# Two attention layers on one core: scores and values in units of eight key chunks, all weights in the common buffer pool

## The chip, the cores and the metric

One core of a Trainium2 chip runs the whole program. The metric is the device time of one execution in microseconds (us), as the median of several runs. The kernel before takes 3022.1 us (three runs, 3020.81 to 3022.92). In the runs made beside the changed kernel and the experiments its median was between 3022.5 and 3023.8 us. All profiles shown are of the fast state, and the verdicts use fast runs alone; the granted TensorE clock of the profiled runs was 0.993 to 0.997.

## The reference, cut to what matters

The input x has 8 batches of 512 channels by 32 x 32 positions, in fp32. Layer one is attention with 8 heads of 64 channels over 1024 positions, after a LayerNorm; layer two has one head of 512 channels, after a GroupNorm.

```
xn = layer_norm(x_flat);  q, k, v = xn @ Wq.T + bq, ...          # 8 heads of 64
attn = softmax(q k^T / 8); x = (attn v) @ Wo.T + bo + x           # layer one
h = group_norm(x, 32 groups)
q, k, v = wq h + bq, wk h + bk, wv h + bv                         # one head of 512
x = x + wp (softmax(q^T k / sqrt(512)) v) + bp                    # layer two
```

## The kernel before

Full matrix products (projections, all of layer two) are done as seven block products with sums of blocks (a Strassen form, `Product`): each step is four or eight recorded TensorE instructions, 1.7 or 3.4 us, with a copy on ScalarE and an addition on VectorE behind some of them. Work that may be done at any time (LayerNorm of the next batch, inversion of the softmax sums, operand differences) lies in a queue, `side`, and `tick()` takes one piece out of it.

The attention of layer one goes by pairs of heads, eight pairs a batch (four pairs, two halves of the queries). A chunk is 128 keys: two heads' scores go to one wide PSUM buffer, of which there are three; ScalarE takes the exp; VectorE adds to the running sum; later the values product reads p. Each matmul of this loop stands in the record as two instructions (16 for the eight of four chunks), so a chunk is four for the scores and four for the values.

```python
groups = [(p, range(g * NM // 2, (g + 1) * NM // 2)) for p in pairs for g in range(2)]   # 4 chunks each
...
for i, (p, ms) in enumerate(groups):
    if i + 1 < len(groups):
        groups[i + 1][0].scores(groups[i + 1][1])
    p.values(ms)
    if i in (4, 8, 12):
        end_pairs(pairs[i // 2 - 2 : i // 2])
...
def scores(self, ms):
    for m in ms:
        s = wide_psum(f"s_{self.tag}_{m}")                 # one of three PSUM buffers
        ... two matmuls, 64x128 tiles ...
        nc.scalar.activation(p, s, AF.Exp, scale=1.0 / float(D) ** 0.5)
        tick()                                             # side work, between the exps
        ... nc.vector.tensor_add(self.sum, self.sum, p)
```

`end_pairs` divides by the sums of two pairs: a small matmul (den), an inversion on VectorE, eight small copies on ScalarE, and two expansions and multiplies on VectorE, all but the matmul by way of `side`:

```python
def invert():  invert_sums(r, compact(t, den))             # VectorE
def copies():                                              # ScalarE, eight copies of 32x16
    for n in range(2):
        for j in range(4):
            nc.scalar.copy(rr[n][ts(j, BL), :], r[ts(2 * n + j // 2, BL), :])
later(invert, copies)
```

At the start, GpSimd makes the block sums of each weight and saves them to DRAM, while VectorE forms `ua`, which layer two needs some 250 us later:

```python
for c in range(NC):
    nc.vector.scalar_tensor_tensor(t, wk[c], 1.0, bq1_row, ALU.mult, ALU.mult, accum_out=ua[:, c : c + 1])
kt = all_of(project("k0", wk_now, bias_of("bk0"), hb))
```

## Time and profile before

| what | value |
|---|---|
| time, median of 3 | 3022.1 us |
| profiled span | 3022.3 us |
| TensorE busy, share of the chain | 99%, 95% |
| VectorE, ScalarE, GpSimd busy | 59%, 35%, 2% |
| one attention stage (first scores to the next projection) | 131.03 us, batches 0 to 6; 131.59 us in batch 7 |
| first V matmul to first scores, batches 1 to 6 | 39.06 us |
| first V matmul of batch 0 | 96.2 us |

How to read it: TensorE's busy share is near one, so its waits say little, and what counts is how long a given stretch of its instructions takes. So the table's last three rows are read from the start times of TensorE's instructions, and I compare them kernel by kernel. The prediction shows the lines. An exp of one chunk takes 1027 ns on ScalarE (mean of 512), and four in a row take 3.77 us.

### The profile page before, as it was taken

To read this page: it belongs to the slowest core of one execution; us is meant where nothing else is said; L and a number is where in the kernel's file an instruction comes from. 1 tells how busy PE (TensorE), PEld (TensorE's weight loads), DVE (VectorE), ACT (ScalarE), POOL (GpSimd) and SP (SyncE) were. 2 spreads that over 40 slices of the span, in tenths; PEclk is the share of its full clock that TensorE was granted. 3 is DMA by queue.
4 is the path that set the end of the run, shared out by engine and by line. 5 is a ranking of instruction groups with operands and counts; after the bars stand their busy time and mean duration, and the time that the engine had idled before them with its cause. 6 is when DMAs were issued, how large, how long until landed. Compare 5 with 4: busy or idle time off the path is not lost.

```text
span 3022.3 us, 26355 instructions
## 1 busy us (share of the span) xinstructions
PE 2984.3 (99%) x10066; PEld 1382.0 (46%) x10066; DVE 1773.9 (59%) x2241; ACT 1045.1 (35%) x1623; POOL 48.9 (2%) x57
## 2 busy tenths in 40 slices
PE   7999999999999999999999999999999999999898
PEld 4533455334553455434553345533455334553344
DVE  6567545674467644675546665466555675436744
ACT  3363213622145221561315512164222642125220
POOL 5000000000000000000000000000000000000000
PEclk8999999999999999999999999999999999999999
DMA  8101331022310313103031041300421013120101
GB/s 292 74 25 35 122 115 70 1 78 79 129 56 1 119 38 136 49 4 129 25 136 49 8 150 45 115 25 11 146 91 70 25 35 122 73 84 8 49 0 57
DMA packets 70760, 217.31 MB, mean 72 GB/s; under 512 B 12832, under 2 KB 16928, under 8 KB 64480
## 3 DMA queue, kind: packets, MB, share of 16 engines
q1 hardware_dynamic: 62176, 204.50, 19.0%
q0 software_dynamic: 2112, 11.01, 0.9%
q8 instruction: 81, 1.33, 0.2%
q10 hardware_dynamic: 6336, 0.03, 0.1%
q14 instruction: 55, 0.45, 0.0%
HBM read 156.26 MB, written 59.24 MB: 71 GB/s over the span
## 4 chain that ended last, share of the span: by engine, by line
PE 95%; DVE 1%; ACT 1%; DMA 0%; issue 0%; SPq 0%; DVEq 0%
PE acc L682 15%; PE s L665 15%; PE x_o L404 5%; PE x_s L396 5%; PE y_s L396 4%; PE y_o L404 4%; PE z_s L396 4%; PE z_o L404 4%; PE x_vm L388 3%; PE x_qa L379 3%; PE x_k L379 3%; PE x_q L379 3%; PE x_v L388 3%; PE x_out L379 2%; PE y_k L379 2%; PE z_k L379 2%
## 5 line engine op out<-in xcount | busy, mean ns | idle before, releaser
L668 ACT ACTIVATE p<-s 128x1024 f32<-128x1024 f32 x512 | 489.1, 1027 | 281.9 <-PE s L665 276.8
L675 DVE TENSOR_TENSOR sum<-sum,p 128x1024 f32<-128x1024 f32 x384 | 469.8, 1223 | 120.8 <-ACT p L668 98.2
L682 PE MATMUL acc<-p,v 128*64 128x512 f32 x2048 | 465.9, 598 | 0.0
L665 PE MATMUL s<-q,k_again 64*128 64x512 f32 x1792 | 416.5, 603 | 1.0 <-ACT p L668 1.0
L682 PEld LDWEIGHTS acc<-p,v 128*64 128x64 f32 x2048 | 136.2, 136 | 315.0 <-issue 290.7
L665 PEld LDWEIGHTS s<-q,k_again 64*128 64x128 f32 x1792 | 163.1, 186 | 252.6 <-issue 197.2
L673 DVE TENSOR_TENSOR sum<-p,p 128x1024 f32<-128x1024 f32 x64 | 78.4, 1225 | 133.5 <-ACT p L668 133.5
L396 PE MATMUL x_s<-S_qa,T_gn 128*128 128x512 f32 x256 | 120.3, 592 | 0.0
L404 PE MATMUL x_o<-T_p,S_vm 128*128 128x512 f32 x256 | 115.1, 592 | 0.0
L767 ACT ACTIVATE p<-p 128x512 f32<-128x512 f32 x128 | 80.7, 630 | 73.1 <-DVE p L318 73.1
L318 DVE TENSOR_TENSOR p<-u(1, 1)_s,y_s 128x512 f32<-128x512 f32 x32 | 22.0, 687 | 132.3 <-ACT u(1, 1)_s L409 132.3
L426 ACT ACTIVATE u(0, 0)_k<-x_k,vecs 128x512 f32<-128x512 f32 x16 | 11.0, 688 | 213.0 <-PE x_k L379 213.0
L685 ACT COPY o<-acc 128x512 f32<-128x512 f32 x64 | 37.5, 586 | 131.7 <-PE acc L682 131.7
L404 PEld LDWEIGHTS x_o<-T_p,S_vm 128*128 128x128 f32 x256 | 48.6, 190 | 61.2 <-issue 61.2
L396 PEld LDWEIGHTS x_s<-S_qa,T_gn 128*128 128x128 f32 x256 | 48.6, 190 | 61.2 <-issue 61.0
L318 DVE TENSOR_TENSOR y<-u(1, 1)_o,y_o 128x512 f32<-128x512 f32 x16 | 11.0, 687 | 101.2 <-ACT u(1, 1)_o L409 101.2
L471 DVE STREAM_TRANSPOSE rden<-rr 128x512 f32<-128x512 f32 (+1 forms) x72 | 55.0, 765 | 19.5 <-ACT rr L821 13.6
L379 PE MATMUL x_out<-T_o,w_o 128*128 128x512 f32 x128 | 61.3, 601 | 3.2 <-DVE T_o L458 3.2
L388 PE MATMUL x_vm<-w_m,T_gn 128*128 128x256 f32 x256 | 60.5, 379 | 0.0
L396 PE MATMUL y_s<-S_qa,gn 128*128 128x512 f32 x128 | 60.2, 592 | 0.0
L396 PE MATMUL z_s<-qa,gn 128*128 128x512 f32 x128 | 60.1, 592 | 0.0
L379 PE MATMUL x_qa<-T_gn,w_a 128*128 128x512 f32 x128 | 60.1, 592 | 0.0
(330 smaller groups left out, 4438.6 us busy)
## 6 DMA issues: line engine op xcount, KB each, us to landing
x<-in_x_dram SPq DMA_DIRECT2D x32, 512.0 KB, 10.3
xr<-in_x_dram SPq DMA_DIRECT2D x64, 256.0 KB, 3.7
x_away<-x SPq DMA_DIRECT2D x32, 512.0 KB, 3.1
x1r<-x_away SPq DMA_DIRECT2D x64, 256.0 KB, 3.3
out_dram<-y SPq DMA_DIRECT2D x64, 256.0 KB, 2.1
w_o<-saved_o SPq DMA_DIRECT2D x8, 1792.0 KB, 7.0
w_a<-saved_a SPq DMA_DIRECT2D x8, 1792.0 KB, 7.1
w_m<-saved_m SPq DMA_DIRECT2D x8, 1792.0 KB, 8.4
```

Source lines behind the costliest of these rows:

```text
L379: nc.tensor.matmul(dst, a[:, k, ts(r, P)], b[:, k, :], start=(opens and k == 0), stop=(k == 1), skip_group_check=True)
L388: nc.tensor.matmul(dst[:, ts(m, CB)], b[:, k, ts(2 * r + m, P)], a[:, k, :], start=(opens and m == 0 and k == 0), stop=(k == 1), skip_grou ...
L396: nc.tensor.matmul(dst, b[:, k, ts(r, P)], a[:, k, :], start=(opens and k == 0), stop=(k == 1), skip_group_check=True)
L404: nc.tensor.matmul(dst, a[:, m, ts(r, P)], b[m // 2][:, m % 2, :], start=(opens and m == 0), stop=(m == NM // 2 - 1), skip_group_check=True)
L471: nc.vector.transpose(t.rearrange("p (k i) -> p k i", i=BL), r.unsqueeze(2).to_broadcast((P, r.shape[1], BL)))
L665: nc.tensor.matmul(s[:, ts(i, HB)], self.k[m // 4][r, ts(m % 4, P)], self.q[r, :], start=True, stop=True)
L668: nc.scalar.activation(p, s, AF.Exp, scale=1.0 / float(D) ** 0.5)
L673: nc.vector.tensor_add(self.sum, self.p[0], p)
L675: nc.vector.tensor_add(self.sum, self.sum, p)
L682: nc.tensor.matmul(self.acc[i * D : (i + 1) * D, :], value_of(self.vt, m, self.c * P + i * D, D), self.p[m][:, ts(i, HB)], start=(m == 0), ...
L685: nc.scalar.copy(self.o, self.acc)
L767: nc.scalar.activation(dest(i, k), dest(i, k), AF.Exp, scale=float(C) ** -0.5)
```

## The change

The intent is to change TensorE between the two tile layouts half as often (eight scores chunks, then eight values chunks), to take side work out from between the exps, and to have one pool for everything. For the longer lead it needs more p tiles, so the weights' own pool is dissolved, and the weights are loaded later in four parts.

```diff
-    wpool = ctx.enter_context(tc.tile_pool(name="wpool", bufs=3))
-    big = ctx.enter_context(tc.tile_pool(name="big", bufs=36))
+    big = ctx.enter_context(tc.tile_pool(name="big", bufs=46))
... (weight tiles, loads and saves in four parts; loads moved: k at pair 1, o at pair 6, a, v and q after later stages)
-                tick()                                   # in Product.step
+                tick(self.pieces)                        # 2 in the query units
... (LayerNorm: the affine steps leave the list of pieces)
             def scores(self, ms):
-                tick()
             def values ...
+                tick()                                   # after each chunk of values
... (main loop)
-            first.scores(range(3))
+            first.scores(range(NM))
             q_last.rest()
-            groups = [...]                               # of four chunks
-            first.scores(range(3, NM // 2))
-            for i, (p, ms) in enumerate(groups):
-                    groups[i + 1][0].scores(groups[i + 1][1])
-                p.values(ms)
+            for i, p in enumerate(pairs):
+                    pairs[i + 1].scores(range(NM))
+                if i < 2 and more:
+                    until(lambda: ln.done)
+                    later(... four ln.affine ...)
+                p.values()
```

More of the change, by code (lines that the diff above doesn't have):

```diff
@@ L185, in put_away, with weight_tiles, saved_part, save_w @@
         return d
-    def slots_of(t):
-        return {n: t[:, i] for i, n in enumerate(SLOTS)}
-    def w_tile(name):
-        return wpool.tile([P, len(SLOTS), 2, CB], F32, tag="w", name=name)
-    def load_w(n, b):
-        t = w_tile(f"w_{n}_{b}")
-        nc.sync.dma_start(out=t, in_=saved[n])
-        return slots_of(t)
-    def sums_of_blocks(engine, w, view=lambda t: t):
-        w = {n: view(t) for n, t in w.items()}
+    def weight_tiles(n):
+        w = {}
+        for g in range(4):
+            t = big_tile(f"w_{n}_{g}").rearrange("p (s a o) -> p s a o", s=2, a=2)
+            for k, name in enumerate((SLOTS + ["21"])[2 * g : 2 * g + 2]):
+                w[name] = t[:, k]
+            w[g] = t
+        return w
+    def saved_part(n, w, g):
+        i, j = 2 * g, min(2 * g + 2, len(SLOTS))
+        return saved[n][:, i:j], w[g][:, : j - i]
+    def load_w(n, b):
+        w = weight_tiles(f"{n}_{b}")
+        for g in range(4):
+            d, t = saved_part(n, w, g)
+            nc.sync.dma_start(out=t, in_=d)
+        return w
+    def save_w(n, w):
+        for g in range(4):
+            d, t = saved_part(n, w, g)
+            nc.gpsimd.dma_start(out=d, in_=t)
+    def sums_of_blocks(engine, w):
         engine.tensor_add(w["S1"], w["21"], w["22"])
@@ L223, in first_w, with complete @@
     def first_w(n):
-        t = w_tile(f"w_{n}_first")
-        w = slots_of(t)
-        w["21"] = half_tile(f"w21_{n}").rearrange("p (a o) -> p a o", a=2)
+        w = weight_tiles(f"{n}_first")
         load_blocks(n + "0", w)
-        def finish(engine):
-            sums_of_blocks(engine, w)
-            nc.gpsimd.dma_start(out=saved[n], in_=t)
-            return w
-        return finish
-    def big_slots(n):
-        w = {}
-        for g in range(4):
-            t = big_tile(f"wb_{n}_{g}").rearrange("p (s a o) -> p s a o", s=2, a=2)
-            for k, name in enumerate((SLOTS + ["21"])[2 * g : 2 * g + 2]):
-                w[name] = t[:, k]
-        return w
-    def save_w(n, w):
-        for i, name in enumerate(SLOTS):
-            nc.gpsimd.dma_start(out=saved[n][:, i], in_=w[name])
-    w_first = {n: first_w(n) for n in ("k", "v", "q")}
-    wo = big_slots("o")
-    load_blocks("o0", wo)
+        return w
+    def complete(n, w):
+        sums_of_blocks(nc.gpsimd, w)
+        save_w(n, w)
+        return w
+    wk_now, wv_now = first_w("k"), first_w("v")
+    wo = first_w("o")
+    wq_now = first_w("q")
     def natural(t, n):
@@ L314, in __init__ @@
             self.behind = []
+            self.pieces = 1
             self.done = 0
@@ L578, in steps @@
                 yield
-                for a in range(2 * (n - 1), 2 * n) if n else ():
-                    self.affine(*blocks[a // 2], a % 2)
-                    yield
-            for a in range(2):
-                self.affine(*blocks[3], a)
-                yield
         def queue(self):
@@ L654, in __init__ @@
             self.sum = None
-            self.acc = None
             if c % 2 == 0:
@@ L675, in scores, with values @@
                     nc.vector.tensor_add(self.sum, self.sum, p)
-        def values(self, ms):
-            if self.acc is None:
-                self.acc = bank(f"acc_{self.tag}")
-            for m in ms:
+        def values(self):
+            acc = bank(f"acc_{self.tag}")
+            for m in range(NM):
                 for i in range(2):
-                    nc.tensor.matmul(self.acc[i * D : (i + 1) * D, :], value_of(self.vt, m, self.c * P + i * D, D),
+                    nc.tensor.matmul(acc[i * D : (i + 1) * D, :], value_of(self.vt, m, self.c * P + i * D, D),
                                      self.p[m][:, ts(i, HB)], start=(m == 0), stop=(m == NM - 1))
-            if m == NM - 1:
-                nc.scalar.copy(self.o, self.acc)
+                tick()
+            nc.scalar.copy(self.o, acc)
     def end_pairs(two):
@@ L886, in fast_path @@
         norm(5)
-        wa = big_slots("a")
+        wa = weight_tiles("a_first")
         product(wa, nq, nk, "a", 0)
@@ L893, in fast_path @@
         norm(100)
+        for k in range(NH):
+            for j in range(2):
+                for a in range(2):
+                    ln.affine(j, k, a)
         hb = operands(ln.result())
@@ L896, in fast_path @@
         until(lambda: not side)
-        wk_now = w_first["k"](nc.gpsimd)
-        wv_now = w_first["v"](nc.gpsimd)
-        sums_of_blocks(nc.gpsimd, wo)
-        save_w("o", wo)
-        wm = big_slots("m")
+        complete("k", wk_now)
+        complete("v", wv_now)
+        complete("o", wo)
+        wm = weight_tiles("m_first")
         product(wm, nv, wp, "m", 0)
@@ L905, in fast_path @@
         product(wm, nv, wp, "m", 1)
-        wq_now = w_first["q"](nc.gpsimd)
-        sums_of_blocks(nc.gpsimd, wa)
-        save_w("a", wa)
-        sums_of_blocks(nc.gpsimd, wm)
-        save_w("m", wm)
+        complete("q", wq_now)
+        complete("a", wa)
+        complete("m", wm)
         for c in range(NC):
@@ L927, in next_values_and_queries @@
             units, q = project(f"q{b}", wq, bias_of("bq0"), hb, True)
+            for u in units:
+                u.pieces = 2
             units[0].rest()
@@ L936, in fast_path @@
             first = Pair(b, 0, 0, qt, kt, vts, ot)
-            first.scores(range(3))
+            first.scores(range(NM))
             q_last.rest()
             pairs = [first] + [Pair(b, hf, c, qt, kt, vts, ot) for hf in range(NH) for c in range(NC) if hf + c > 0]
-            groups = [(p, range(g * NM // 2, (g + 1) * NM // 2)) for p in pairs for g in range(2)]
-            first.scores(range(3, NM // 2))
-            for i, (p, ms) in enumerate(groups):
-                if i + 1 < len(groups):
-                    groups[i + 1][0].scores(groups[i + 1][1])
-                p.values(ms)
-                if i in (4, 8, 12):
-                    end_pairs(pairs[i // 2 - 2 : i // 2])
-                if i == 2 and more:
+            for i, p in enumerate(pairs):
+                if i + 1 < len(pairs):
+                    pairs[i + 1].scores(range(NM))
+                if i < 2 and more:
+                    until(lambda: ln.done)
+                    later(*(lambda j=j, a=a, i=i: ln.affine(j, i, a) for j in range(2) for a in range(2)))
+                if i == 1 and more:
                     wk_next = load_w("k", b + 1)
-                if i == 3:
-                    wo_now, wa_now = load_w("o", b), load_w("a", b)
-                if i == 11 and more:
-                    until(lambda: ln.done)
+                if i == 6:
+                    wo_now = load_w("o", b)
+                if i == 7 and more:
                     hb = operands(ln.result())
                     add_operands(hb)
+                p.values()
+                if i in (2, 4, 6):
+                    end_pairs(pairs[i - 2 : i])
             if more:
@@ L962, in fast_path @@
                 k_units[0].rest()
+            wa_now = load_w("a", b)
             ob = operands(ot)
@@ L988, in fast_path @@
                 u.rest()
-            if more:
-                wv_next, wq_next = load_w("v", b + 1), load_w("q", b + 1)
             whole = Whole(b, qa, h1b, x1_away)
@@ L1010, in fast_path @@
                 all_checks()
+            if more:
+                wv_next, wq_next = load_w("v", b + 1), load_w("q", b + 1)
             o_units = whole.values(vm)
```

## The prediction

> **What bounds the kernel now.** I first read the page's busy times and the chain that ended last.
>
> ```profile
> PE 2984.3 (99%) x10066; PEld 1382.0 (46%) x10066; DVE 1773.9 (59%) x2241; ACT 1045.1 (35%) x1623; POOL 48.9 (2%) x57
> ...
> PE 95%; DVE 1%; ACT 1%; DMA 0%; issue 0%; SPq 0%; DVEq 0%
> ```
>
> TensorE holds 95% of the chain and has only 38 us without a record. The other engines have slack. So the change can gain only by shortening TensorE's own work or its waits. Next the waits of TensorE, longest first, each with total, times and longest:
>
> ```profile
> PE pst_q L260 <- DMA w_q<-in_L_conv_wq_dram: 6.1, 2, 5.1
> PE z_k L379 <- ACT wb_m L274: 4.3, 1, 4.3
> PE var L525 <- DVE lnq L502: 4.1, 1, 4.1
> ...
> PE s L665 <- ACT p L668: 1.1, 7, 0.2
> ```
>
> The large ones occur once, at the start. In the attention loop only seven waits of 0.16 us (1.1 us) repeat. There is thus almost no wait to take away. What is left is TensorE time that no wait shows. For that I read its instructions in order of time, in the middle of batch 3:
>
> ```profile
> 1294.25 3.70 PE L665 MATMUL s<-q,k_again 64*128 64x512 f32 x16
> 1297.88 3.65 PE L682 MATMUL acc<-p,v 128*64 128x512 f32 x16
> 1301.47 3.70 PE L665 MATMUL s<-q,k_again 64*128 64x512 f32 x16
> 1305.10 3.65 PE L682 MATMUL acc<-p,v 128*64 128x512 f32 x16
> 1308.69 3.70 PE L665 MATMUL s<-q,k_again 64*128 64x512 f32 x16
> ```
>
> Four key chunks are 16 recorded instructions (two heads[...]). From start to start, a scores group takes 3.63 us and a values group 3.59 us. Now the last two values groups of batch 1, which already stand together:
>
> ```profile
> 625.80 7.09 PE L682 MATMUL acc<-p,v 128*64 128x512 f32 x32
> 632.82 1.98 PE L379 MATMUL x_k<-x,w_k 128*128 128x512 f32 x4
> ```
>
> 32 values instructions take 632.82 - 625.80 = 7.02 us, not 2 x 3.59 = 7.18: joining saved 0.16 us. For scores, the chain has one run of 20 in batch 7 (4.49 us): four instructions more than 16 cost 4.49 - 3.63 = 0.86, that is 0.215 each, so 16 should cost 3.44 and a run pays 0.19 us for being entered. A round trip values-scores-values costs about 0.35 us.
>
> [...] Scores are a 64x128 layout, values 128x64[...], with 0.16 to 0.19 us per boundary. [...] The trace has 1027 ns, and four in 3.77 us, so one per (3.77 - 1.02)/3 = 0.917 us. [...]
>
> **The change part by part.**
>
> *Units of eight.* Before, a batch has 16 values groups, the last two adjacent: 15 runs, and the timeline has 15 in each of the eight batches. Scores come as runs of 3, 5, then fourteen of 4: 16 runs. The order of the built program after the change has scores 8, query unit, scores 8, then values 8 and scores 8 in turn; the last two values units have a denominator between them. That is 8 scores entries instead of 16 and 8 values entries instead of 15; the denominators' own entries stay as many. Saved per batch: 8 x 0.19 + 7 x 0.16 = 2.64 us, in eight batches 21.1 us, all on the path, since TensorE is the chain. The matmul count doesn't change.
>
> *ScalarE's pace in a unit of eight.* There are three wide PSUM buffers for scores. TensorE makes a chunk every 4 x 0.214 = 0.855 us, ScalarE frees one every 0.917. In a unit of four this hardly shows; in eight it accumulates. Around one unit of before:
>
> ```profile
> 1295.49 3.77 ACT L668 ACTIVATE p<-s 128x1024 f32<-128x1024 f32 x4 [0.48 <-PE s L665]
> ...
> 1296.07 0.19 PEld L665 LDWEIGHTS s<-q,k_again 64*128 64x128 f32 x2 [0.24 <-issue]
> ...
> 1296.56 0.19 PEld L665 LDWEIGHTS s<-q,k_again 64*128 64x128 f32 x2 [0.29 <-ACT p L668]
> 1296.93 0.19 PEld L665 LDWEIGHTS s<-q,k_again 64*128 64x128 f32 x2 [0.18 <-issue]
> ```
>
> The weight load of the fourth chunk came 0.06 us late because of the first exp, and the next was on time, so the matmuls lost nothing. Load pairs stand 0.43 us apart and take 0.19, so about 0.2 us of lateness is absorbed. Lateness grows by 0.917 - 0.855 = 0.062 us per chunk: 0.06, 0.12, 0.18, 0.25, 0.31 for chunks four to eight. The last exceeds 0.2 by 0.1 us. I take 0.1 us x 64 units = 6 us given back. This is the least certain term; 0 to 13 us (0.2 each) is possible.
>
> *Side work.* The LayerNorm of the next batch now ends in the query units, two pieces a step, and its affine runs on ScalarE during values units. This takes eight affines of 0.81 us out from between the exps, so the 1.1 us of waits above goes. In exchange the variance matmul stands inside a query unit (two mode changes instead of one, about 0.15 us x 7 = 1 us). The scaling of x on VectorE (1.22 us each) also stands between outputs of the query units, whose PSUM buffers are then freed late: by adding durations in the new order, z of the second query unit becomes free within some tenths of a microsecond of its need. I take 0.2 us x 8 = 1.5 us.
>
> *VectorE's sums.* Seven adds at 1.30 us (four in 5.21) make 9.1 us per pair, within about 14 us of TensorE work. The next batch's T operands move from the sixth pair to the last values unit. Added up from the end of the seventh pair: denominator 1.05, inversion 1.5, eight small copies 1.7, two expands and two scalings 2.8, two T 2.5, so the T needed first is there after about 9 us, and TensorE wants it after 1 + 7 + 3.4 = 11.4. No wait.
>
> *Weights.* The bytes are the same, in four DMAs instead of one 1792 KB load that landed in 7 to 8 us. In the built program they wait on buffers freed a pair or a stage ahead of use, tens of us. Hidden. At the start VectorE's multiplies cost 3.3 us instead of 1.22 while GpSimd is busy, in both kernels; GpSimd's instructions are as many, reordered. I take 0, plus or minus 3 us.
>
> Sum: 3022.1 - 21.1 - 1.1 + 6 + 1 + 1.5 = 3008.4 us.
>
> **The rivals.** (1) ScalarE becomes the pace of each scores unit. For it: 0.917 against 0.855 us, three buffers. Against: 0.2 us of slack in the loads, and ScalarE rests in each values unit, so the debt is paid off every 14 us. If the whole excess of 0.31 us stalled TensorE in 64 units, 20 us would be lost and the kernel would land near 3020. (2) A late buffer or DMA. The big pool now holds p tiles, operands and weights[...]. For it: already before, a residual load stands on the chain in some batches, and the w_m loads now stand between the residual loads. Against: the order shows the earliest residual loads ahead of them still, and the late ones have about 10 us against 4 for landing and 5 for the megabyte ahead. Were it 4 us in each batch, the result would be near 3039. (3) The whole gain arrives, with nothing given back: 3022.1 - 22.2 = 3000. (4) VectorE lags by more than a pair and denominators wait: its 89 us busy in 131 us of attention stage speak against it; 2 us per batch would give 3023.
>
> **Range and chances.** The saving of 22 us rests on measured boundaries and is only 0.7%. Give-backs from 2 to 16 us and the start's 3 us, either way, make 2999 to 3019. For 2% the time would have to fall by 60 us, which no part contains, or rise by 60, which only rival 2 at 7 us per batch could do.
>
> **What would show it.** Right: acc and s appear in runs of 32; TensorE's sum of s and acc in time falls; pairs stand 13.9 to 14.1 us apart (without denominator) instead of 14.44; waits of s on p are short but in many units; the span of one attention stage falls from 131 to about 129 us. Wrong: waits of TensorE on p above 0.2 us per unit (rival 1), on x or w with a DMA behind (rival 2), on sum (rival 4), or a run of 32 that takes twice a run of 16, so that no boundary cost was there.

## The result

The changed kernel takes 3011.22 us (median of 4 runs, 3009.59 to 3013.5) against 3022.51 us of the kernel before in the same rounds. The ratio is 0.9962, with an interval of 0.9945 to 0.998. A ratio is the mean time of one kernel's fast runs over that of the other's of the same rounds, so it is not quite the ratio of the medians. The profiled span is 3008.7 us, 13.6 us less than before.

The page of the changed kernel, busy times and chain:

```profile
PE 2965.4 (99%) x10066; PEld 1385.9 (46%) x10066; DVE 1787.4 (59%) x2241; ACT 1035.2 (34%) x1623; POOL 47.9 (2%) x57
...
PE 93%; DVE 3%; DMA 2%; issue 1%; ACT 0%; SPq 0%; DVEq 0%; ACTq 0%
```

TensorE has as many instructions as before and is busy 18.9 us less (2984.3 - 2965.4): the same work took less time. VectorE's share of the chain has risen from 1 to 3%. The longest two waits of TensorE (total, times, longest) say where. (The 2% of DMA are loads at the start and, in most batches, a late load of a piece of the residual, xr, of about 4 us each; see rival 2 below.)

```profile
PE z_k L378 <- DVE k L317: 14.6, 1, 14.6
PE pst_q L258 <- DMA w_q<-in_L_conv_wq_dram: 6.0, 2, 5.0
```

The second was there before. The first is new. It occurs once, at the start. The waits of scores on p are gone from this list, which is that of the matmuls; the weight loads have a list of their own, shown below.

TensorE in time, batch 1 (start, duration, line, operation): two runs from the middle of the stage and two from near its end.

```profile
550.53 7.14 PE L657 MATMUL s<-q,k_again 64*128 64x512 f32 x32
557.60 7.09 PE L672 MATMUL acc<-p,v 128*64 128x512 f32 x32
...
609.02 7.42 PE L657 MATMUL s<-q,k_again 64*128 64x512 f32 x32
616.37 7.09 PE L672 MATMUL acc<-p,v 128*64 128x512 f32 x32
```

Runs are now of 32. From start to start, scores take 7.07 us (557.60 - 550.53) where two runs of 16 took 2 x 3.63 = 7.26. But the second scores run takes 7.35. It is one of two long ones in each batch (7.24 and 7.35). No wait of a matmul is listed for either. ScalarE beside both runs shows the reason:

```profile
551.76 7.44 ACT L660 ACTIVATE p<-s 128x1024 f32<-128x1024 f32 x8 [0.54 <-PE s L657]
...
608.35 1.71 ACT L694 COPY rr<-r 32x16 f32<-32x16 f32 x8 [4.74 <-DVE r L631]
610.08 0.59 ACT L675 COPY o<-acc 128x512 f32<-128x512 f32 x1
610.57 7.45 ACT L660 ACTIVATE p<-s 128x1024 f32<-128x1024 f32 x8
```

Normally the exps begin 1.23 us after the scores (551.76 - 550.53). Here they begin 1.55 us after (610.57 - 609.02). Ahead of them stand the eight small copies, which waited 4.74 us for VectorE's inversion r, and the copy of acc. The inversion stood behind VectorE's sums of the next pair.

The pace of the exps is not invisible, but it stands with the weight loads (PEld), which wait for the PSUM buffer ahead of the matmuls. Their list of waits has one entry for it, and the loads of the run at 550.53 show what it is made of (idle time before the load in brackets):

```profile
PEld s L657 <- ACT p L660: 137.4, 320, 1.0
...
552.84 0.19 PEld L657 LDWEIGHTS s<-q,k_again 64*128 64x128 f32 x2 [0.30 <-ACT p L660]
...
556.50 0.33 PEld L657 LDWEIGHTS s<-q,k_again 64*128 64x128 f32 x4 [0.53 <-ACT p L660]
```

320 is five in each of the 64 units. Load pairs lie 0.43 us apart when nothing holds them up. Against that grid the first load of chunk four comes 0.06 us late, and those of chunks five to eight 0.12, 0.18, 0.24 and 0.30 us; the run still takes 7.07 us. In the run of 7.35 us the last chunk's load (at 615.31) is 0.61 us late, and 0.28 us of it is paid. So 0.30 us of lateness is absorbed in the first run and 0.33 in the second.

The start of each batch tells how the 13.6 us came about. At the first V matmul of batch 0 the changed kernel is 3.4 us late. It is 0.9 us late at batch 1, then 1.2, 3.0, 5.0, 7.5, 9.7 and 11.3 us early at batches 2 to 7. The attention stages take 128.37 to 128.38 us in batches 0 to 4 and 128.74, 128.72 and 129.43 us in the last three: 20.0 us less in all eight. The stretch from the first V matmul to the first scores takes 39.40 us, 0.34 us more, in seven batches. So the terms are -20.0 (stages), +2.4 (LayerNorm beside the queries, 7 x 0.34), +3.4 (start), and +0.7 us for the rest, mainly the stretch around the output projection, where single batches differ by up to 0.45 us either way.

The start is the surprise. VectorE in the kernel before, one of the four instructions that form `ua`:

```profile
74.15 1.67 DVE L913 SCALAR_TENSOR_TENSOR uat<-w_k,bq_row 128x512 f32<-128x512 f32 x1
```

And the changed kernel, with GpSimd and TensorE beside it:

```profile
66.16 4.84 DVE L904 SCALAR_TENSOR_TENSOR uat<-w_k,bq_row 128x512 f32<-128x512 f32 x1
...
67.97 1.26 POOL L215 TENSOR_TENSOR w_q_first<-w_q_first,w_q_first 128x512 f32<-128x512 f32 x1
...
70.39 1.10 POOL L210 DMA_DIRECT2D saved_q<-w_q_first  x2
...
81.19 3.78 PE L378 MATMUL z_k<-T_h,w_k_first 128*128 128x512 f32 x4 [14.58 <-DVE k L317]
```

The first K projection begins 6.5 us earlier than before (57.87 against 64.37 us). TensorE does not wait directly ahead of it in either kernel. The largest part was won earlier, at the variance, where the kernel before had this wait, which the changed kernel doesn't have:

```profile
42.71 1.97 PE L525 MATMUL var<-lnq,ones_c 128*64 128x512 f32 x2 [4.06 <-DVE lnq L502]
```

The sum lnq ahead of it took 4.17 us on VectorE beside GpSimd's sums, and takes 0.68 us now. It too ended only after GpSimd had gone over from three sums to issuing a DMA. (VectorE's four multiplies by rstd are faster too, 7.28 us against 13.24.) But then the four `ua` instructions take 4.24 to 4.84 us each, where one took 0.68 us undisturbed in the kernel before. Each ends 0.61 us after GpSimd has gone over from three sums to issuing DMAs. The K outputs stand behind them, and TensorE waits 14.6 us.

The start is not steady from one execution to the next. Seven of the experiments below leave its code as it is. In their profiles and the changed kernel's own, the first V matmul starts at 95.3 to 100.7 us, 98.8 on average, with 8.9 to 14.6 us of this wait. Of the kernel before there is one profile, with 96.2 us. So the +3.4 us is the difference of one pair of profiles; against the mean of the eight it is 2.6.

### The profile page after: what moved, and what is told of

Its sections match the earlier page's. It is cut to its first block, busy times and chain, and to the rows that moved or that the text cites. A ratio compares the mean times of both kernels' runs of the same rounds, so it can differ in the third digit from the quotient of the medians.

```text
span 3008.7 us, 26701 instructions
## 1 busy us (share of the span) xinstructions
PE 2965.4 (99%) x10066; PEld 1385.9 (46%) x10066; DVE 1787.4 (59%) x2241; ACT 1035.2 (34%) x1623; POOL 47.9 (2%) x57
## 3 DMA queue, kind: packets, MB, share of 16 engines
q8 instruction: 81, 1.33, 0.2%
## 4 chain that ended last, share of the span: by engine, by line
PE 93%; DVE 3%; DMA 2%; issue 1%; ACT 0%; SPq 0%; DVEq 0%; ACTq 0%
PE s L657 15%; PE acc L672 14%; PE x_o L403 5%; PE x_s L395 5%; PE y_s L395 4%; PE y_o L403 4%; PE z_o L403 4%; PE z_s L395 4%; PE x_q L378 3%; PE x_vm L387 3%; PE x_qa L378 3%; PE x_v L387 3%; PE x_k L378 3%; PE y_k L378 2%; PE y_q L378 2%; PE z_qa L378 2%
## 5 line engine op out<-in xcount | busy, mean ns | idle before, releaser
L660 ACT ACTIVATE p<-s 128x1024 f32<-128x1024 f32 x512 | 476.3, 1057 | 85.2 <-PE s L657 85.2
L672 PE MATMUL acc<-p,v 128*64 128x512 f32 x2048 | 453.6, 595 | 0.0
L657 PE MATMUL s<-q,k_again 64*128 64x512 f32 x1792 | 403.3, 600 | 0.3
L694 ACT COPY rr<-r 32x16 f32<-32x16 f32 x256 | 51.6, 202 | 102.5 <-DVE r L631 99.4
L395 PE MATMUL x_s<-qa,gn 128*128 128x512 f32 x128 | 60.2, 592 | 0.0
```

Of the source, the lines that this page charges most:

```text
L395: nc.tensor.matmul(dst, b[:, k, ts(r, P)], a[:, k, :], start=(opens and k == 0), stop=(k == 1), skip_group_check=True)
L657: nc.tensor.matmul(s[:, ts(i, HB)], self.k[m // 4][r, ts(m % 4, P)], self.q[r, :], start=True, stop=True)
L672: nc.tensor.matmul(acc[i * D : (i + 1) * D, :], value_of(self.vt, m, self.c * P + i * D, D), self.p[m][:, ts(i, HB)], start=(m == 0), stop ...
```

## The experiments

All are edits of the changed kernel, and all gave correct results. Unless said otherwise "stage" is the attention stage of batches 1 to 4.

**Units of four, all else kept.** Theory: the gain is the mode boundaries (the changes between the two tile layouts). Rival: it is the side work or the loads.

```diff
-                p.values()
+                p.values(range(0, 4))
+                if i + 1 < len(pairs): pairs[i + 1].scores(range(4, 8))
+                p.values(range(4, 8))          # and scores(range(0, 4)) ahead; first.scores(range(NM)) stays
```

> The changed kernel with one thing undone: scores and values of eight chunks are emitted in turns of four again (the lead of eight chunks, the weights, the LayerNorm, everything else stay). Theory (the gain is the mode boundaries): each batch gets 7 more scores entries at 0.19 us and 7 more values entries at 0.16 us, 2.45 us a batch, 19.6 us in all: about 3031 us against 3011 of the changed kernel, attention stage about 130.8 us against 128.4. Should the late copies' stalls (0.45 us a batch) go with the shorter units, 3.6 us less: 3027. Rival (the gain came from the side work moved out from between the exps, or from the weights' loads): within 3 us of 3011, attention stage near 128.4.

Measured: 3041.7 us (3037.08 to 3045.06), ratio 1.0065 (1.0051 to 1.0078); stage 132.50 us. The rival that the gain lies elsewhere is out (its bounds were 3 us and a stage of 128.4), but the loss is 4.1 us a batch and not 2.5. The wait view lists 12.5 us of scores waiting for p, in 16 waits, two a batch. ScalarE at one of them:

```profile
574.69 1.71 ACT L697 COPY rr<-r 32x16 f32<-32x16 f32 x8 [3.03 <-DVE r L631]
576.42 3.77 ACT L660 ACTIVATE p<-s 128x1024 f32<-128x1024 f32 x4
```

The scores had begun at 573.92, so the exps are 2.5 us behind. The same late copies that cost the units of eight 0.45 us a batch thus cost the units of four at least 1.56, by the list (against a run below that differs in the copies alone it is 132.50 - 130.40 = 2.1 us). The comparison mixed two effects, and it was repeated below with the copies in time.

**The ua instructions behind the first K projection.**

```diff
-        for c in range(NC): ... scalar_tensor_tensor(t, wk[c], 1.0, bq1_row, ...)
         kt = all_of(project("k0", wk_now, bias_of("bk0"), hb))
+        for c in range(NC): ... scalar_tensor_tensor(t, wk[c], 1.0, bq1_row, ...)
```

> The changed kernel with four VectorE instructions (weight times bias row, summed into ua, which is needed only in the second layer) moved from in front of the first K projection to behind it. In the changed kernel they took 4.2 to 4.8 us each while GpSimd worked, and TensorE waited 14.6 us for the K output behind them. Theory: that wait goes, nothing as long takes its place; the first V projection starts at 83 to 86 us instead of 99.6, and the kernel falls by 12 to 16 us, to 2995 to 2999. Rival: the K outputs on VectorE are stretched by GpSimd in the same way (a third wait takes its place): 5 us or less gained, 3006 or more.

Measured: 2993.25 us (2991.54 to 2994.69), ratio 0.9901 (0.9886 to 0.9916), 18.0 us less than the changed kernel where 12 to 16 were expected. The first V matmul starts at 83.45 us, within the expected 83 to 86, so 16.2 us of it lie at the start. GpSimd is as busy as before while the K outputs are written:

```profile
69.44 1.27 POOL L216 TENSOR_TENSOR w_q_first<-w_q_first,w_q_first 128x512 f32<-128x512 f32 x1
...
69.83 0.69 DVE L317 TENSOR_TENSOR k<-u(1, 0)_k,z_k 128x512 f32<-128x512 f32 x1 [0.38 <-PE z_k L378]
```

The K output takes 0.69 us right beside a GpSimd sum. It reads one operand from SBUF and one from PSUM; a `ua` instruction reads two from SBUF, and beside such sums it took 4.84 us in the changed kernel. The sum lnq, a TENSOR_TENSOR of 128x512 like the K output, reads two as well and took 4.17 us beside them in the kernel before. That the second operand from SBUF makes the difference is my reading of these. Put behind the K projection and GpSimd's sums, the `ua` instructions take 0.68 or 0.69 us.

**The inversion ahead of the next pair's sums.**

```diff
                     end_pairs(pairs[i - 2 : i])
+                    tick()                    # emits the inversion now, the copies stay in the next values
```

> The changed kernel with the inversion of the sums put on VectorE ahead of the next pair's sums rather than behind them, so that ScalarE's eight small copies are ready to run at once after the exps. Theory: the runs of 32 scores that took 7.24 and 7.35 us (pair indices 5 and 7) take 7.07 us again, 0.45 us a batch, 3.6 us in all: about 3007.6 against 3011.2; the attention stage 127.9 to 128.0 us instead of 128.4. Rival: those runs are long for another reason (the plain pace of the exps): no change, 3011.

Measured: 3004.81 us (3003.84 to 3009.32), ratio 0.9941 (0.9928 to 0.9955); stage 127.94 us, as expected. ScalarE and TensorE around the pair that took 7.35:

```profile
604.51 1.70 ACT L694 COPY rr<-r 32x16 f32<-32x16 f32 x8
...
609.90 7.14 PE L657 MATMUL s<-q,k_again 64*128 64x512 f32 x32
```

The copies no longer wait. They run just after the exps, during the values, and the run of 32 takes 7.06 us again. The stages of the two profiles account for 4.3 us: 0.45 to 0.48 in six batches, and 0.80 in batches 5 and 6, where the long run had taken 7.70 us. The median fell by 6.4, more than they explain. The other 2.1 us are within the spread of both kernels' runs, 4 and 5 us; with the start repaired as well (last run below) the early inversion brings 3.8.

**One piece of side work a query step instead of two.**

```diff
-                u.pieces = 2
+                u.pieces = 1
```

> The changed kernel with one piece of side work for each step of the query units instead of two, which puts the variance matmul back between the first query unit and the scores. Theory: the stretch from the first V matmul to the first scores falls from 39.4 us to the 39.06 of the kernel before, 0.34 us in each of seven batches, 2.4 us in all: about 3008.8. Rival: the end of the LayerNorm, now later, delays the first pair's sums or outputs of the second query unit, and 1 to 3 us come back there: 3010 to 3013.

Measured: 3013.42 us (3012.51 to 3016.33), ratio 0.9969 (0.9957 to 0.9982). Theory and rival both came true. The stretch to the first scores is 39.06 us again. But the stage is 129.17 to 129.18 us, 0.8 us longer in seven batches, because the rest of the LayerNorm now stands behind the first pair's sums on VectorE. In one batch:

```profile
521.25 1.98 PE L378 MATMUL y_q<-x,w_q 128*128 128x512 f32 x4 [0.24 <-DVE q L317]
```

The net is a loss of 0.46 us a batch. The two pieces a step were the better choice.

**Units of four and of two, with the early inversion.** Now only the boundaries differ from the run with the early inversion alone (3004.8 us, stage 127.94).

> Units of four together with the early inversion (which takes the waits of scores on late exps out: 1.56 us a batch with units of four, 0.45 with units of eight), to be compared with the early inversion alone (3004.8 us, attention stage 127.94 us). Theory (only the mode boundaries are left): 7 more scores and 7 more values entries a batch at 0.35 to 0.36 us the pair, 2.5 us a batch: stage 130.4 us, about 3025 us. Rival (short units lose to something else as well, as the first run with units of four, 4.1 us a batch, could be read): stage 131.0 us or more, 3030 us or more.

> Units of two with the early inversion: 21 more scores and 21 more values entries a batch than with units of eight. Theory of a fixed price for each boundary: 21 x 0.36 = 7.5 us a batch, stage 135.4 us, about 3064 us, three times the loss of units of four; up to 1 us a batch more if the eight small copies of 1.7 us now hold an exp back. Rival (the gain is not in the boundaries but saturates): less than twice the loss of units of four.

Measured, units of four: 3026.09 us (3020.28 to 3030.48, 13 runs), ratio 1.0008 (1.0 to 1.0016); stage 130.40, which is 2.46 us more. Units of two: 3063.43 us (3060.59 to 3063.63), ratio 1.0129 (1.0113 to 1.0144); stage 135.32, which is 7.38 us more. Per added pair of entries that is 2.46 / 7 = 0.351 us and 7.38 / 21 = 0.351 us. The price of a boundary is fixed and doesn't saturate. In units of two it can be read off the timeline:

```profile
1304.96 1.99 PE L657 MATMUL s<-q,k_again 64*128 64x512 f32 x8
1306.88 1.94 PE L674 MATMUL acc<-p,v 128*64 128x512 f32 x8
1308.74 1.99 PE L657 MATMUL s<-q,k_again 64*128 64x512 f32 x8
```

Scores and values of two chunks take 3.78 us from start to start (1308.74 - 1304.96); a quarter of the 14.08 us of eight chunks (7.06 + 7.02) would be 3.52. The difference of 0.26 is three quarters of 0.351, as it must be when four such rounds hold three more boundary pairs than one.

**Exps put back on purpose.** Two small copies ahead of each pair's first exp, with the early inversion.

```diff
+                if m == 0:
+                    for n in range(2):
+                        nc.scalar.copy(p[:BL, ts(n, BL // 2)], s[:BL, ts(n, BL // 2)])
                 nc.scalar.activation(p, s, AF.Exp, scale=1.0 / float(D) ** 0.5)
```

> Early inversion, and two small ScalarE copies (32 partitions, 16 columns, about 0.21 us each) put in front of the first exp of each pair, so that the eight exps of each of 64 units run 0.43 us later. It measures how much slack a run of 32 scores has against ScalarE. My reading of the runs of 7.24 and 7.35 us (exps 0.20 and 0.32 us later than usual cost 0.17 and 0.28 us) is that almost none is left, 0.03 to 0.07 us: each unit then loses 0.36 to 0.40 us, stage 127.94 + 2.9 to 3.2 = about 131 us, the kernel 23 to 26 us slower than the early inversion alone, about 3029 us. Rival (weight loads and buffers absorb such lateness, ScalarE is far from the bound): under 5 us slower, 3010 us or less.

Measured: 3017.19 us (3014.48 to 3020.54, 17 runs), ratio 0.9978 (0.9971 to 0.9986); stage 129.26 us. It is 12.4 us slower than the early inversion alone (10.6 by the stages, 8 x 1.33), half of what I expected and more than twice what the rival allows.

```profile
552.73 0.23 ACT L662 COPY p<-s 32x16 f32<-32x16 f32 x2 [0.47 <-PE s L657]
552.98 7.44 ACT L663 ACTIVATE p<-s 128x1024 f32<-128x1024 f32 x8
```

The two copies took 0.23 us together, not 0.43. The scores began at 551.55, so the exps begin 1.43 us after them instead of 1.24, 0.19 later, and the run takes 7.23 us instead of 7.06, 0.17 longer. My dose was wrong; the reading of the slack was right: 0.19 - 0.17 = 0.02 us, about the size to which these starts can be read. The long runs of the changed kernel give nearly the same: exps that begin 1.43 and 1.55 us after the scores instead of 1.23 cost 0.17 and 0.28 us, which leaves 0.03 and 0.04 us.

**Side work between the scores' chunks again, units of eight.**

```diff
                 self.p[m] = p
+                tick()                        # in scores
...
-                tick()                        # in values, except in the last pair
```

> The changed kernel with the side work given out between the scores' chunks again, as in the kernel before, rather than between the values' chunks (the last pair, which has no scores behind it, keeps it in its values). Units stay at eight. Theory (a run of 32 scores has only about 0.08 us of slack against ScalarE, so whatever ScalarE does between the first five exps is paid in full): four LayerNorm affines of 0.74 us in each of two pairs cost 2 x (2.97 - 0.08) = 5.8 us a batch in seven batches, 40 us; two blocks of eight copies (1.71 us) cost 3.3 us a batch, 26 us, of which the 3.6 us that they cost already go off: about 63 us slower than the changed kernel, 3074 us. Moving the side work would then be what makes units of eight possible at all. Rival (such work between the exps costs what it cost in the kernel before, seven waits of 0.16 us and little else): under 10 us slower, below 3021.

Measured: 3071.33 us (3066.51 to 3072.96), ratio 1.0154 (1.0137 to 1.0171), slower than either kernel and 60 us slower than the changed one, where the theory said 63. In a run of 32 scores with four affines between the exps, ScalarE and TensorE read:

```profile
549.48 0.81 ACT L549 ACTIVATE x<-x,vecs 128x512 f32<-128x512 f32 x1
550.19 1.02 ACT L660 ACTIVATE p<-s 128x1024 f32<-128x1024 f32 x1
...
551.26 1.13 PE L657 MATMUL s<-q,k_again 64*128 64x512 f32 x4 [0.48 <-ACT p L660]
```

Exp and affine alternate, and each chunk of scores waits for a buffer. The run takes from 545.78 to 555.55, 9.77 us instead of 7.06. Work on ScalarE between the exps is paid nearly in full in a unit of eight: four affines put the exps 1.61 us apart instead of 0.92, 2.76 us in all, and the run is 2.71 us longer. Only the units could thus not have been changed alone: the side work had to move into the values.

**Both repairs together**, the `ua` instructions behind the K projection and the early inversion.

> Both repairs together: the four VectorE instructions behind the first K projection, and the inversion ahead of the sums. Theory (independent causes, one at the start, one in the attention stage): 2993.3 - 3.6 = about 2989.7 us, stage 127.94 us, first V projection at 83 to 84 us. Rival (they share slack): no better than 2993.

Measured: 2989.44 us (2989.08 to 2990.24), ratio 0.9886 (0.9871 to 0.9901); stage 127.93 us. It is 34 us faster than the kernel before on the same rounds (3023.62) and about 22 us faster than the changed kernel. The wait list of TensorE now begins with the load of the first weight at the very start:

```profile
PE pst_q L258 <- DMA w_q<-in_L_conv_wq_dram: 6.0, 2, 5.2
PE x_out L378 <- DVE T_o L457: 3.2, 1, 3.2
```

## Why the prediction was right, point by point

The time (3008, range 2999 to 3019) holds the 3011.22 us, and the class "within 2%" is right. By its steps:

- **Units of eight, -21.1 us. Right.** 0.35 us for a scores and a values entry was read from two places of the old trace; the two dose runs measured 0.351. The stage fell by 131.03 - 128.38 = 2.65 us a batch against the step's 2.64. That these agree as they stand is in part luck: the removed waits and the long runs, the next two points, cancel (0.44 us each).
- **Removed waits, -1.1 us. Right in kind, too small.** The step took the wait list at its word. The timeline of the kernel before, batch 3, shows the first run of 20 scores after the queries:

```profile
1248.65 3.70 PE L665 MATMUL s<-q,k_again 64*128 64x512 f32 x16
1252.52 1.13 PE L665 MATMUL s<-q,k_again 64*128 64x512 f32 x4 [0.16 <-ACT p L668]
1253.58 3.65 PE L682 MATMUL acc<-p,v 128*64 128x512 f32 x16
```

  The whole run of 20 took 4.93 us there (1253.58 - 1248.65), against 4.49 us in batch 7, which has no LayerNorm behind it. So the affines between the exps cost 0.44 us a batch, of which the list shows 0.16: 3.1 us in seven batches, not 1.1.
- **ScalarE's pace, +6 us (0.1 us in each of 64 units). The mechanism was right, the slack mis-sized.** The lateness of the loads in a unit of eight is what the step said, 0.06 to 0.30 us against 0.06 to 0.31. But about 0.33 us of it is absorbed and not 0.2, so with its exps on time a run of 32 takes 7.06 to 7.07 us, and nothing is lost; 0.02 to 0.04 us are left at the end of a run. (The exp's 1027 and 917 ns, which the step used, are those of the traces.) What is lost is lost in two runs a batch, where the small copies make the exps late: 0.45 us a batch, 3.6 us in all. That the inversion would stand behind the sums, and the copies behind it, I had overlooked.
- **Variance and scaling in the query units, +2.5 us. The sum came, 0.34 us in seven batches, 2.4 us, but by luck.** The second query unit, for which the step charged 1.5 us, takes 12.27 us in the changed kernel and 12.26 before: nothing is lost there. All of it lies in the first unit, charged with 1 us. About 0.2 us a batch stand in the steps on either side of the variance, a matmul of 128x64 tiles among those of 128x128: they take 1.81 and 1.82 us from start to start instead of 1.72 (in batch 1). The step's 0.15 us for one more mode change was an estimate, near the 0.16 to 0.19 us read per boundary. The other 0.14 stand in the unit's last two steps, without a listed wait; why is not shown.
- **Weights hidden. Right**: both waits of TensorE on a DMA in the list are of the first weights at the start. **The start, 0 plus or minus 3 us: +3.4 us**, or 2.6 against the mean start of eight profiles, so at the edge of what was allowed. The size hides two large effects of opposite sign, the start's earlier K projection (-6.5) and the new wait behind it (+14.6 in place of the 4.3 that z_k waited before). The step noted that GpSimd slows VectorE's multiplies to 3.3 us "in both kernels" (in the changed kernel it was 7.28 / 4 = 1.82) and stopped there. It didn't ask which of them would now meet GpSimd's sums: the `ua` instructions, with the K outputs behind them.

Summed up as measured: -21.1 - 3.1 + 3.6 + 2.4 + 3.4 = -14.8 us, and the profiled span fell by 13.6. What is between them lies in two stages of 128.7 instead of 128.4 us (0.7 us; the last long run took 7.70 us there instead of 7.35, while the run with the `ua` instructions moved has the same attention code and 128.4 in both) and around the output projection (0.7 us), less some rounding. I did not pursue these two. The terms missed by 2 to 3.4 us each in both directions, so that the sum came as near as it did is luck.

Of the rivals, (1) was nearer than I thought: ScalarE doesn't set the pace, but the run with side work between the exps shows it does as soon as 0.02 to 0.04 us are used up. (2) came in a small size: y_out's waits for x, with the late load of xr on the chain ahead of them, rose from three (1.2 us) to six (1.7 us), and in the experiments' profiles they are 1.9 to 2.6 us. No wait on a weight is in the attention loop. (4) left no wait in the list. (3), the whole gain, is what the repaired kernel gets and exceeds. Of the signs named in advance, runs of 32, pairs 14.09 us apart and a stage of about 129 us came. The "short but many" waits of scores on p came too, 320 of them, with the weight loads and not with the matmuls.

Small slips of the prediction: of the waits of 2.4 to 4.3 us that are called "at the start", three (x_out, x_qa, pm) stand in the last batch. From its own sum of 3008.4, rival 2 gives 3040 and rival 4 gives 3024, not 3039 and 3023. And 2% more than the kernel before would take about 9 us a batch, not 7. None of them bears on the range.

## What to carry to other kernels

Price a boundary between TensorE layouts from a place in the old trace where two runs already stand together; the price, 0.351 us for a change and back, held here from units of two to units of eight. When waits are read, read those of the weight loads as well as those of the matmuls (here 320 on p, where the matmuls' list has none). When a producer gets longer runs through a few buffers, its consumer must be left alone during the run (with four affines between the exps a run took 9.77 us instead of 7.06): look for what stands ahead of the consumer's first instruction, and what that waits for on a third engine. And before VectorE work with two SBUF inputs is left in front of something urgent (the `ua` instructions took 0.68 us undisturbed and 4.24 to 4.84 us beside GpSimd's sums), see what GpSimd is doing at that time.

## What else the runs show, and what they leave open

- A change from 128x64 to 64x128 tiles and back cost 0.351 us, the same in units of two and of four (against eight).
- A `ua` instruction of the changed kernel stood on VectorE over three GpSimd sums in a row (1.26 us each) and took 4.84 us instead of 0.68; it ended only after GpSimd went on to issue DMAs. In the kernel before, three `ua` instructions took 1.67 to 1.89 us each, 1.0 to 1.2 us more than undisturbed, beside GpSimd sums of 1.28 to 2.24. What decides between the two is not shown. The K outputs, with one operand from SBUF, took 0.69 us beside GpSimd's sums (the run with the `ua` instructions moved).
- Here a wait for a PSUM buffer stood with the weight load and did not show at the matmul: runs of 32 scores grew from 7.07 to 7.35 us without a wait of a matmul, while the weight loads' list has 320. In the kernel before 0.44 us were lost where the matmuls' list had 0.16. Comparing the lengths of equal runs showed it.
- Two copies of 32x16 from PSUM took 0.23 us together, while eight copies of the same size, from SBUF, took 1.71 us, 0.21 for each. What makes the difference is not shown.
